# Moving a quad's attention scores behind the last block of attention's products in a gated cross-attention kernel, with dense 32x32 transposes and the gate bias added in DRAM

## The chip, the cores and the metric

The kernel runs on one core of a Trainium2 chip. The metric is device time in microseconds of the whole launch. Before the change it is 980.86 us, the median of three runs (980.78 to 980.89).

## The reference

Eight batches of 1024 tokens with 1024 features (`x`) attend to 64 memory rows of 512 features each. All is float32.

```python
memory_proj    = einsum('bme,de->bmd', memory, W_mem)            # 8 x 64 x 1024
scores         = einsum('bnd,bmd->bnm', x, memory_proj) / sqrt(1024)
attn           = softmax(scores, axis=-1)
memory_context = einsum('bnm,bmd->bnd', attn, memory_proj)
gate           = sigmoid(einsum('bnf,df->bnd', concat([x, memory_context]), W_gate) + b_gate)
fused          = x + gate * memory_context
out            = fused * rsqrt(mean(fused**2, -1) + 1e-6) * norm_w
```

Most of the work is the first half of the gate: x times a 1024 x 1024 weight, for 8192 tokens. The second half is small in another form: memory_context times W2 is attn times (memory_proj times W2), so the kernel computes `mg = memory_proj W2` once (512 x 1024), adds the bias to it (rows of attn sum to one), and multiplies attn by it.

## The kernel before, in words

**Stages.** A start of about 84 us loads the weights, projects the memory (`pm`), computes mg in seven block products (`mg_product`), and stores memory_proj and mg in two DRAM tensors, `mpd` and `mgd`. Then the tokens go through in 16 *quads* of 512 tokens, two a batch. A quad takes about 55 us.

**A quad.** x of the quad is loaded (`load_xq`) and transposed in blocks of 32x32 on VectorE (`transpose_x`), into four tiles A11, A12, A21, A22 of 256 tokens by 512 features. The 512 x 1024 by 1024 x 1024 product is then done by a fast scheme of seven block products in place of eight, on two levels. On the outer level VectorE forms sums S1 to S4 of the A tiles (`outer_s`); S3 is formed in place of A21. Each of the seven *blocks* is again seven *products* A, B, C, D, A, E, F (A has two parts), for which GpSimd forms four sums (`inner_s`). A product is two float32 matmuls, and the profile shows each as two records. So a quad has 49 products, one for each *slot*. VectorE and GpSimd add products into the `gate` tiles.

**Attention.** Scores of a quad (`scores`) are 16 float32 matmuls with 64 stationary columns each, two of them side by side on the array (tile psT, 32 records). ScalarE copies them to `sT`, TensorE turns them back (`transpose_scores`), softmax runs in two parts (`softmax_a`, `softmax_b`), and the result is turned once more (`transpose_attn`). Four of the seven blocks, those of outer products 5, 4, 2 and 3, are *extended*: after their second A product come eight matmuls of 64 rows, two side by side, with attn as the stationary side. They give memory_context (`pc`) and add mg's part of the gate to the block's sums (kA, kD, kE, kF). Sigmoid, gated product, residual (a DMA that adds x), and the norm follow.

**Order of the work.** Every engine's instructions stay in the order in which the program issues them (`pin`). That order is made by hand: `at(slot, fn)` issues a piece of work just before the product of a slot, `mid((quad, block), fn)` issues it inside a block, after its second A product and its extension, and ahead of the adds of that block and of product E (the loop over `beside` in `outer_product`). `plan(q)` fills in both. The blocks run in the order of `ORDER`: 1, 6, 7, 5, 4, 2, 3; the last number of a bracket says which half of the mg rows is used.

```python
ORDER = ((1, None), (6, None), (7, None), (5, (1, 1, 2)), (4, (1, 0, 2)), (2, (0, 0, 0)), (3, (0, 1, 4)))
SLOTS = 49
```

So block 1 has slots 0 to 6, block 6 slots 7 to 13, and block 3, the last, slots 42 to 48. In the kernel before, the scores of a quad and S3, S4 are issued at its slot 7, between blocks 1 and 6; S1 and S2 of the next quad in the middle of block 3.

**PSUM.** The products of a block use five banks that rotate from block to block (`banks`): a bank written in one block is written again, in the next block, four or more products after the matmuls that filled it, and must have been read by then. The extension's pc tiles have two banks of their own, and psT, the scores turned back and attn turned back share one (tag `sc`).

**Layout.** Token tiles are loaded so that a partition holds 32 tokens' quarter rows. In the kernel before, feature chunk j of a token holds features j, j + 8, j + 16, ...: `chunks` reads them with a step of eight floats, and the rows of both gate weights and the columns of W_mem are taken in the same way (`rows_by_chunk`, `chunks`).

**Bias.** mg's rows for a batch come back from `mgd` by `load_mg`; for each batch `add_bias` then adds b_gate to one half of them in SBUF, with a DMA from GpSimd's queue.

Of the kernel before, what the change touches and what calls it, by code (L numbers as in the profile page):

```python
# [10 lines left out]
ALU = mybir.AluOpType  # L11
# [4 lines left out]
P = 128  # L16
# [4 lines left out]
def tile_gated_cross_attention_rmsnorm(  # L21
# [38 lines left out]

    nc = tc.nc
    B, N, D = x.shape
    M, E = mem.shape[1:]
    QT = 4 * P
    QPB = N // QT
    NQ = B * QPB
    BM = B * M  # L70
    KD = D // P
    KE = E // P
    H = 512
    C = 256
    NPAIR = BM // P
# [6 lines left out]
    apool = ctx.enter_context(tc.tile_pool(name="apool", bufs=1))  # L82
# [6 lines left out]
    pin = tc.keep_in_program_order  # L89
# [7 lines left out]
    def load(o, i):  # L97
        pin(nc.sync.dma_start(o, i))

    def t4k(pool, shape, tag, name):  # L100
        return pool.tile(shape, F32, tag=tag, name=name)

    def rows_by_chunk(w, n):

        return w.rearrange("(p j) f -> p j f", j=n)

    def chunks(t, n):

        return t.rearrange("p s e -> p (s e)").rearrange("p (m j) -> p j m", j=n)

    banks = [f"b{i}" for i in range(5)]

    def bank(n, shape, name):
        return ps.tile(shape, F32, tag=banks[n % 5], name=name)
# [10 lines left out]
    memq = [t4k(rot, [P, 2, E], "l2", f"memq{i}") for i in range(2)]  # L125
    wm = t4k(xqpool, [P, KE, D], "xq", "wm")
    wmr = w_mem_t.rearrange("(k p) d -> p k d", p=P)
# [2 lines left out]
        load(memq[g], memr[g])  # L130
    load(wm[:, 1, :], wmr[:, 1, :])
    load(wm[:, 2:, :], wmr[:, 2:, :])
    w2r = rows_by_chunk(w_gate_t[D:, :], KD)
    w2 = []
    for k in range(KD):
        t = t4k(*((gpool, [P, D], "gate") if k < 7 else (apool, [P, D], "s4")), f"w2_{k}")
        load(t, w2r[:, k, :])
        w2.append(t)

    w1 = [const.tile([P, 4, D], F32, name=f"w1_{h}") for h in range(2)]
    for h in range(2):
        load(w1[h], rows_by_chunk(w_gate_t[:D, :], KD)[:, 4 * h : 4 * h + 4, :])
    nw_sb = const.tile([P, D], F32, name="nw_sb")
    load(nw_sb, norm_w.partition_broadcast(P))
    xq = {}

    def load_xq(q):
# [7 lines left out]
    outer_b = {  # L157
        o: w1[h][:, :, c * H : (c + 1) * H]
        for o, h, c in ((1, 0, 0), (7, 0, 1), (2, 1, 0), (3, 1, 1))
# [24 lines left out]
    mgd = dram.tile([2, BM, D], F32, name="mgd")  # L184
    memT = [t4k(rot, [P, 2, BM], "u", f"memT{i}") for i in range(2)]

    def transpose_mem(g):

        cols = slice(g * (BM // 2), (g + 1) * (BM // 2))
        for k in range(KE):  # L190
            for r in range(2):
                n = 2 * g + r
                pin(
                    nc.tensor.transpose(
                        pt[k][:, n * P : (n + 1) * P], memq[g][:, r, k * P : (k + 1) * P], ident
                    )
                )
            o = memT[k // 2][:, k % 2, cols]
            pin((nc.scalar.copy if k % 2 else nc.vector.tensor_copy)(o, pt[k][:, cols]))

    pt = [bank(4, [P, BM], "pt0")]
    pt += [ps_ctx.tile([P, BM], F32, tag="ctx", name=f"pt{k}") for k in (1, 2)]
    pt += [ps.tile([P, BM], F32, tag="sc", name="pt3")]
    for g in range(2):
        transpose_mem(g)
    pm = [bank(j, [P, BM], f"pm{j}") for j in range(5)]
    pm += [ps_ctx.tile([P, BM], F32, tag="ctx", name=f"pm{j}") for j in (5, 6)]
    pm += [ps.tile([P, BM], F32, tag="sc", name="pm7")]
    for k in range(KE):
        for j in range(KD):  # L210
            mm(
                pm[j],
                chunks(wm[:, k : k + 1, :], KD)[:, j],
                memT[k // 2][:, k % 2, :],
                k == 0,
                k == KE - 1,
            )
# [16 lines left out]
    A, S, L2, O = {}, {}, {}, {}  # L234
    sTs, attns, attnTs, scs, mps, mgs = {}, {}, {}, {}, {}, {}
# [3 lines left out]
    def transpose_x(q, t, half):  # L239

        key = q, t // 2, half
        if key not in A:
            A[key] = t4k(
                apool, [P, KH, 2 * P], f"a{t // 2 + 1}{half + 1}", f"a{t // 2 + 1}{half + 1}_{q}"
            )
        r = t % 2
        pin(
            nc.vector.transpose(  # L248
                A[key][:, :, r * P : (r + 1) * P],
                chunks(xq[q][:, 4 * t : 4 * t + 4, :], KD)[:, half * KH : (half + 1) * KH],  # L250
            )
        )

# [114 lines left out]
        for g in range(2):  # L368
            load(mgs[b][g * M : (g + 1) * M, :], mgd[g, b * M : (b + 1) * M, :])

    def add_bias(b):
        pin(nc.gpsimd.dma_start(mgs[b][M:P, :], b_gate.partition_broadcast(M), accum_op=ALU.add))

    KH = KD // 2
    HM = BM // 2
    b11, b12, b21, b22 = (
        [w2[h * KH + k][:, c * H : (c + 1) * H] for k in range(KH)]
# [17 lines left out]
    mpT = [[t4k(apool, [P, KH, HM], f"a{r + 1}{h + 1}", f"mpT{r}{h}") for h in range(2)] for r in range(2)]  # L397
# [14 lines left out]
    def store_mp(g):  # L412

        r, n = g // 2, g % 2
        mpq = const.tile([P, 4, Q4], F32, tag=f"it{(4, 6, 2, 3)[g]}", name=f"mpq{g}")
        for h in range(2):
            pin(
                nc.vector.transpose(
                    chunks(mpq, KD)[:, h * KH : (h + 1) * KH],
                    mpT[r][h][:, :, n * P : (n + 1) * P],  # L420
                )
            )
        for i in range(4):
            load(
                mgd[0, g * P : (g + 1) * P, i * Q4 : (i + 1) * Q4].rearrange(
                    "(s c) e -> c s e", c=32
                ),
                mpq[32 * i : 32 * (i + 1), :, :],
            )
# [16 lines left out]
    def mg_tile(pool, tag, name):  # L446
        return t4k(pool, [P, 2, H], tag, name)

# [10 lines left out]
    s1 = mp_step(nc.vector, "s1", apool, m21, m22, ALU.add)  # L459
    s2 = mp_step(nc.vector, "s2", apool, s1, m11, ALU.subtract)  # L460
# [59 lines left out]
    def at(slot, fn, *args):  # L520
        due.setdefault(slot, []).append(lambda: fn(*args))

    def mid(key, fn, *args):
        beside.setdefault(key, []).append(lambda: fn(*args))
# [5 lines left out]
    def plan(q):  # L530
        t0 = SLOTS * q
        nxt = q + 1 < NQ
        order = [o for o, _ in ORDER]
        for i, o in enumerate(order):
            for part, t in ((0, 1), (1, 5)):
                if i + 1 < len(order):
                    at(t0 + 7 * i + t, inner_s, q, order[i + 1], part)
                elif nxt:
                    at(t0 + 7 * i + t, inner_s, q + 1, order[0], part)
        at(t0 + 7, scores, q)  # L540
        at(t0 + 7, outer_s, q, 3)
        at(t0 + 7, outer_s, q, 4)
        at(t0 + 9, transpose_scores, q)
        at(t0 + 10, softmax_a, q)
        at(t0 + 13, softmax_b, q)
        at(t0 + 18, transpose_attn, q)
        at(t0 + 21, attn_difference, q)
        if not nxt:
            at(t0 + 5, load_last)
            return  # L550
        at(t0 + 2, load_xq, q + 1)
        for t in (2, 3):
            mid((q, 5), transpose_x, q + 1, t, 0)
            mid((q, 2), transpose_x, q + 1, t, 1)
        for i, t, half in ((36, 0, 0), (38, 1, 0), (43, 0, 1), (45, 1, 1)):
            at(t0 + i, transpose_x, q + 1, t, half)
        mid((q, 3), outer_s, q + 1, 1)
        mid((q, 3), outer_s, q + 1, 2)
        if (q + 1) % QPB == 0:
            at(t0 + 10, load_mp, (q + 1) // QPB)  # L560
            at(t0 + 49, load_mg, (q + 1) // QPB)
        if q % QPB == 0:
            at(t0 + 8, add_bias, q // QPB)

    for o in (2, 3):
        w1_place(o)
# [102 lines left out]
    def outer_product(q, o, ext):  # L669
# [3 lines left out]
        s1, s2, s3, s4 = (L2[q, o][:, i, :, :] for i in range(4))  # L673
# [64 lines left out]
        if ext:  # L738
            row, h, g = ext
# [43 lines left out]
        if o in (4, 3) and q + 1 == NQ:  # L783
            c, d = 2 * ext[0], 2 * ext[0] + 1
            if o == 3:
                sqrt_table()
            first = (4, 5) if o == 4 else (3, 3)
            at(slot + first[0], last_root, d)
            at(slot + first[1], last_root, c)
            for i, t in enumerate((d, c)):  # L790
                for h_ in range(2):
                    at(slot + first[1] + 1 + 2 * i + h_, last_norm, t, h_)
        elif o in (4, 3):

            row = ext[0]
            c, d = 2 * row, 2 * row + 1
            for t in (d, c):
                at(slot + 5, residual, q, t)
            if row == 0:
                when = (17, 18, 23, 29, None, None)  # L800
            else:
                when = (17, 18, 23, 25, 26, 28)
            at(slot + when[0], square, q, c)
            at(slot + when[1], square, q, d)
            for w_, (t, h_) in zip(when[2:], ((c, 0), (c, 1), (d, 0), (d, 1))):
                if w_ is None:
                    mid((q + 1, 4), norm, q, t, h_)
                else:
                    at(slot + w_, norm, q, t, h_)
# [36 lines left out]
```

## Time and profile before

| what | value |
|---|---|
| time | 980.86 us (980.78 to 980.89) |
| span of the profiled execution | 979.4 us |
| granted TensorE clock | 0.996 |
| VectorE: transposes of x | 128 of 128x512, 1098 ns each, 137.9 us |
| VectorE: S3 in place of A21 | 16, idle 23.2 us before them |
| TensorE: psT | 512 records, from quad to quad 55.05 us apart |
| GpSimd: bias | 8 DMAs of 256 KB, 847 ns of GpSimd each |
| DMA | 128.32 MB, 131 GB/s over the span |

How to read it: PE is TensorE's matmuls, PEld its weight loads, DVE VectorE, ACT ScalarE, POOL GpSimd, SP the engine that issues most DMAs. A group is a line of the code with its tiles, how many instructions it has, their busy time, the mean of one in ns, and the idle time of the engine just before them. Matmul ends are modelled in the profile and neighbours overlap, so for TensorE the times from start to start say more than busy time. `64*128` in a TensorE line is the tile of the array in use: rows by columns.

### The profile page before, as it was taken

What the parts mean: (1) busy time and instruction counts of PE and PEld (TensorE: products, weight loads), DVE (VectorE), ACT (ScalarE), POOL (GpSimd) and SP (SyncE); (2) the same over time, 40 slices, a digit from 0 to 9 for tenths busy, and PEclk for the clock granted to TensorE, in tenths of its full rate; (3) what the DMA queues carried; (4) which work ended last, traced back from release to release, by engine and by line L of the source; (5) the groups of instructions that cost most, each with busy time, mean ns of one, the idle gap of its engine ahead of it and who ended that gap; (6) DMA issues with size and microseconds to landing.
All of it is one profiled execution on the core that took longest, in us unless ns stands there. A gap on an engine that the chain in (4) does not pass through costs nothing.

```text
span 979.4 us, 14277 instructions
## 1 busy us (share of the span) xinstructions
PE 964.8 (99%) x4938; PEld 769.8 (79%) x4938; DVE 820.4 (84%) x1487; ACT 324.9 (33%) x602; POOL 730.5 (75%) x881
## 2 busy tenths in 40 slices
PE   9999999999999999999999999999999999999995
PEld 6546888888887888888887888888887888888873
DVE  3888788979797988979797988979797988979787
ACT  1100234151433334151433334151433334151434
POOL 3366877878787877878787877878787877878772
PEclk9999999999999999999999999999999999999998
DMA  9865264482918374482918374482818364482612
GB/s 372 258 153 145 39 120 107 103 188 62 186 65 165 108 141 106 102 190 65 183 65 164 111 138 105 107 184 66 182 65 168 110 136 104 108 184 68 169 65 86
DMA packets 71255, 128.32 MB, mean 131 GB/s; under 512 B 12432, under 2 KB 49296, under 8 KB 70928
## 3 DMA queue, kind: packets, MB, share of 16 engines
q1 hardware_dynamic: 61760, 93.34, 35.3%
q0 software_dynamic: 9280, 33.56, 18.5%
q8 instruction: 39, 0.64, 0.3%
q10 hardware_dynamic: 144, 0.52, 0.2%
q14 instruction: 32, 0.26, 0.1%
HBM read 87.56 MB, written 39.85 MB: 130 GB/s over the span
## 4 chain that ended last, share of the span: by engine, by line
PE 96%; DVE 2%; DMA 1%; issue 0%; ACT 0%; POOL 0%; DVEq 0%; ACTq 0%
PE kA L92 20%; PE pc L92 12%; PE kE L92 11%; PE kF L92 10%; PE kD L92 10%; PE kC L92 10%; PE kB L92 10%; PE psT L92 6%; PE pg L92 5%; PE pm L92 3%; DVE gate L95 1%; DMA memq<-in_mem 1%; DVE gate L660 0%; PE pa L342 0%; PE sc L316 0%
## 5 line engine op out<-in xcount | busy, mean ns | idle before, releaser
L95 POOL TENSOR_TENSOR gate<-gate,u 128x256 f32<-128x256 f32 x336 | 270.4, 835 | 115.7 <-DVE u L95 110.1
L582 ACT ACTIVATE gate<-gate 128x512 f32<-128x512 f32 x128 | 79.0, 629 | 400.1 <-DVE gate L95 400.1
L95 POOL TENSOR_TENSOR l<-a 128x256 f32<-128x256 f32 x128 | 128.9, 1007 | 60.4 <-DVE a L95 55.8
L248 DVE STREAM_TRANSPOSE a<-xq 128x512 f32<-128x512 f32 x128 | 137.9, 1098 | 4.0 <-DMA xq<-in_x 4.0
L92 PE MATMUL pc<-mg,attnT 64*128 64x256 f32 x512 | 127.4, 389 | 0.0
L611 DVE SCALAR_TENSOR_TENSOR gate<-gate,ss,nw_sb 128x512 f32<-128x512 f32 x120 | 126.0, 1060 | 1.1
L92 PE MATMUL kD<-it,l 128*128 128x256 f32 x448 | 115.0, 379 | 0.0
L92 PE MATMUL kB<-it,l 128*128 128x256 f32 x448 | 115.0, 379 | 0.0
L92 PEld LDWEIGHTS pc<-mg,attnT 64*128 64x128 f32 x512 | 90.6, 186 | 29.7 <-issue 21.2
L92 PE MATMUL kA<-w,a 128*128 128x256 f32 x384 | 98.7, 379 | 0.4 <-ACT u L726 0.4
L92 PEld LDWEIGHTS kD<-it,l 128*128 128x128 f32 x448 | 85.1, 190 | 11.6
L92 PEld LDWEIGHTS kB<-it,l 128*128 128x128 f32 x448 | 85.1, 190 | 11.6
L95 DVE TENSOR_TENSOR gate<-gate,pc 128x512 f32<-128x512 f32 x128 | 87.0, 680 | 5.8 <-ACT gate L582 5.8
L95 POOL TENSOR_TENSOR l<-s 128x256 f32<-128x256 f32 x96 | 75.7, 789 | 10.8 <-PE kF L92 10.7
L92 PEld LDWEIGHTS kA<-w,a 128*128 128x128 f32 x384 | 71.6, 190 | 10.2 <-ACT u L726 0.8
L726 ACT COPY u<-kA 128x256 f32<-128x256 f32 x112 | 40.5, 362 | 102.1 <-PE kA L92 99.9
L92 PE MATMUL kE<-it,a 128*128 128x256 f32 x256 | 69.0, 392 | 0.0
L95 DVE TENSOR_TENSOR u<-u,kB 128x256 f32<-128x256 f32 x112 | 45.5, 406 | 28.1 <-PE kB L92 24.9
L92 PE MATMUL kA<-t,s 128*128 128x256 f32 x256 | 67.4, 386 | 0.0
L92 PE MATMUL kC<-w,l 128*128 128x256 f32 x256 | 65.7, 379 | 0.0
L92 PE MATMUL kF<-w,l 128*128 128x256 f32 x256 | 65.7, 379 | 0.0
L596 ACT ACTIVATE junk<-gate 128x1024 f32<-128x1024 f32 x60 | 63.5, 1059 | 2.1 <-DMA gate<-in_x 1.2
(123 smaller groups left out, 1996.6 us busy)
## 6 DMA issues: line engine op xcount, KB each, us to landing
xq<-in_x SPq DMA_DIRECT2D x64, 512.0 KB, 9.6
gate<-in_x POOLq DMA_DIRECT2D x60, 512.0 KB, 7.8
out<-gate SPq DMA_DIRECT2D x60, 512.0 KB, 2.6
w<-in_w_gate_t SPq DMA_DIRECT2D x8, 512.0 KB, 11.0
w<-in_w_gate_t SPq DMA_DIRECT2D x2, 2048.0 KB, 15.6
mg<-mgd SPq DMA_DIRECT2D x16, 256.0 KB, 4.0
mpd<-mpT SPq DMA_DIRECT2D x4, 512.0 KB, 3.8
mgd<-mpq SPq DMA_DIRECT2D x16, 128.0 KB, 2.6
```

The source lines that it names most:

```text
L92: pin(nc.tensor.matmul(o, lhsT, rhs, start=start, stop=stop, skip_group_check=True))
L95: pin(eng.tensor_tensor(o, a, b, op))
L248: nc.vector.transpose(A[key][:, :, r * P : (r + 1) * P], chunks(xq[q][:, 4 * t : 4 * t + 4, :], KD)[:, half * KH : (half + 1) * KH],)
L582: pin(nc.scalar.activation(g, g, AF.Sigmoid))
L596: nc.scalar.activation(junk, O[q, t], AF.Square, accum_out=ss[:, t % 2 : t % 2 + 1])
L611: nc.vector.scalar_tensor_tensor(g[:, cols], g[:, cols], rstd[:, t % 2 : t % 2 + 1], nw_sb[:, cols], ALU.mult, ALU.mult,)
L726: pin(nc.scalar.copy(p1, kb["A"]))
```

## The change

The change has five parts:

1. *Scores.* For quads 1 to 15 the scores are issued inside block 3 of the quad before, right behind attention's matmuls there. Quad 0 keeps them at slot 7. S3 and S4 go from slot 7 to slots 5 and 6 (but for quad 0).
2. *Dense blocks.* Feature chunk j becomes 32 features in a row out of each quarter of 256. `blocks` and `tokens` then read and write runs of 32 floats in both kinds of transposes (of x and of memory_proj). The gate weights' rows are loaded in that order: w2 in eight loads as before, w1 in eight of 512 KB where it was two of 2 MB. The columns of W_mem are put in order by four copies on VectorE (`order_wm`), from which the projection then reads its stationary side.
3. *Bias.* For batch 0 it is added as before. For batches 1 to 7 one DMA adds it to the 448 rows of `mgd`, in quad 0 at slot 20.
4. *Transposes.* Two of the eight transposes of the next quad go from slots 43 and 45 to 42 and 43.
5. *Norms.* The last two norm halves of the row finished in block 4 go from 26 and 28 to 29 and 32 slots after it, which are slots 15 and 18 of the next quad.

Parts 1, 4 and 5 set the order on TensorE and VectorE, part 2 is meant to make VectorE's transposes read and write dense memory, and part 3 is to take issues off GpSimd.

```diff
-    def rows_by_chunk(w, n):
-        return w.rearrange("(p j) f -> p j f", j=n)
-    def chunks(t, n):
-        return t.rearrange("p s e -> p (s e)").rearrange("p (m j) -> p j m", j=n)
+    def rows_by_chunk(w):
+        return w.rearrange("(i j r) f -> i r j f", i=4, r=32)
+    def blocks(t, half):
+        return t.rearrange("p s (j r) -> p s j r", r=32)[:, :, half * KH : (half + 1) * KH, :]
+    def tokens(t):
+        return t.rearrange("p j (s c) -> p s j c", c=32)
...
-    for h in range(2):
-        load(w1[h], rows_by_chunk(w_gate_t[:D, :], KD)[:, 4 * h : 4 * h + 4, :])
+    for k in range(KD):
+        load(w1[k // KH][:, k % KH, :], w1r[:, :, k, :])
...
+    def order_wm(k):
+        t = t4k(apool, [P, KD, P], ("a11", "a12", "s1", "s2")[k], f"wmp{k}")
+        pin(
+            nc.vector.tensor_copy(
+                t.rearrange("p j (i r) -> p j i r", r=32),
+                wm[:, k, :].rearrange("p (i j r) -> p j i r", i=4, r=32),
+            )
+        )
+        wmp.append(t)
+    order_wm(0)
     for g in range(2):
         transpose_mem(g)
+    for k in range(1, KE):
+        order_wm(k)
...
             nc.vector.transpose(
-                A[key][:, :, r * P : (r + 1) * P],
-                chunks(xq[q][:, 4 * t : 4 * t + 4, :], KD)[:, half * KH : (half + 1) * KH],
+                tokens(A[key][:, :, r * P : (r + 1) * P]),
+                blocks(xq[q][:, 4 * t : 4 * t + 4, :], half),
             )
...
-        at(t0 + 7, scores, q)
-        at(t0 + 7, outer_s, q, 3)
-        at(t0 + 7, outer_s, q, 4)
+        if q == 0:
+            at(t0 + 7, scores, q)
+        at(t0 + (5 if q else 7), outer_s, q, 3)
+        at(t0 + (6 if q else 7), outer_s, q, 4)
...
-        for i, t, half in ((36, 0, 0), (38, 1, 0), (43, 0, 1), (45, 1, 1)):
+        for i, t, half in ((36, 0, 0), (38, 1, 0), (42, 0, 1), (43, 1, 1)):
             at(t0 + i, transpose_x, q + 1, t, half)
+        mid((q, 3), scores, q + 1)
         mid((q, 3), outer_s, q + 1, 1)
         mid((q, 3), outer_s, q + 1, 2)
...
-        if q % QPB == 0:
-            at(t0 + 8, add_bias, q // QPB)
+        if q == 0:
+            at(t0 + 8, add_bias, mgs[0][M:P, :])
+            at(t0 + 20, add_bias, mgd[1, M:, :])
...
-                when = (17, 18, 23, 25, 26, 28)
+                when = (17, 18, 23, 25, 29, 32)
```

More of the change, by code (lines that the diff above doesn't have):

```diff
@@ L72, in tile_gated_cross_attention_rmsnorm @@
     KE = E // P
+    KH = KD // 2
     H = 512
@@ L132, in tile_gated_cross_attention_rmsnorm @@
     load(wm[:, 2:, :], wmr[:, 2:, :])
-    w2r = rows_by_chunk(w_gate_t[D:, :], KD)
+    w2r = rows_by_chunk(w_gate_t[D:, :])
     w2 = []
@@ L136, in tile_gated_cross_attention_rmsnorm @@
         t = t4k(*((gpool, [P, D], "gate") if k < 7 else (apool, [P, D], "s4")), f"w2_{k}")
-        load(t, w2r[:, k, :])
+        load(t, w2r[:, :, k, :])
         w2.append(t)
     w1 = [const.tile([P, 4, D], F32, name=f"w1_{h}") for h in range(2)]
-    for h in range(2):
-        load(w1[h], rows_by_chunk(w_gate_t[:D, :], KD)[:, 4 * h : 4 * h + 4, :])
+    w1r = rows_by_chunk(w_gate_t[:D, :])
+    for k in range(KD):
+        load(w1[k // KH][:, k % KH, :], w1r[:, :, k, :])
     nw_sb = const.tile([P, D], F32, name="nw_sb")
@@ L203, in tile_gated_cross_attention_rmsnorm @@
     pt += [ps.tile([P, BM], F32, tag="sc", name="pt3")]
+    wmp = []
+    def order_wm(k):
[8 more added lines that the diff above has]
+    order_wm(0)
     for g in range(2):
         transpose_mem(g)
+    for k in range(1, KE):
+        order_wm(k)
     pm = [bank(j, [P, BM], f"pm{j}") for j in range(5)]
@@ L212, in tile_gated_cross_attention_rmsnorm @@
                 pm[j],
-                chunks(wm[:, k : k + 1, :], KD)[:, j],
+                wmp[k][:, j, :],
                 memT[k // 2][:, k % 2, :],
@@ L369, in load_mg, with add_bias @@
             load(mgs[b][g * M : (g + 1) * M, :], mgd[g, b * M : (b + 1) * M, :])
-    def add_bias(b):
-        pin(nc.gpsimd.dma_start(mgs[b][M:P, :], b_gate.partition_broadcast(M), accum_op=ALU.add))
-    KH = KD // 2
+    def add_bias(rows):
+        pin(
+            nc.gpsimd.dma_start(
+                rows, b_gate.partition_broadcast(rows.shape[0]), accum_op=ALU.add
+            )
+        )
     HM = BM // 2
@@ L418, in store_mp @@
                 nc.vector.transpose(
-                    chunks(mpq, KD)[:, h * KH : (h + 1) * KH],
-                    mpT[r][h][:, :, n * P : (n + 1) * P],
+                    blocks(mpq, h),
+                    tokens(mpT[r][h][:, :, n * P : (n + 1) * P]),
                 )
```

## The prediction

> **What bounds the kernel now.** I read the page first (busy times, the chain that ended last), then TensorE's waits, then TensorE's timeline in one quad of the middle, and last the groups and the timeline of the engines that the change relieves. The page's busy row and the chain:
>
> ```profile
> PE 964.8 (99%) x4938; PEld 769.8 (79%) x4938; DVE 820.4 (84%) x1487; ACT 324.9 (33%) x602; POOL 730.5 (75%) x881
> ...
> PE 96%; DVE 2%; DMA 1%; issue 0%; ACT 0%; POOL 0%; DVEq 0%; ACTq 0%
> ```
>
> TensorE is the chain. Busy ends are modelled, so I asked its waits too. They come to 3.9 us in all; the largest:
>
> ```profile
> PE kA L92 <- ACT u L726: 1.6, 3, 1.1
> ```
>
> Three waits, all in the last quad. The psT groups of quads 1 to 15 start at 145.77, 200.81, 255.86, ... us: 55.05 us apart every time. So each quad is as long as TensorE's own stream, and only what shortens that stream, or makes it wait, moves the time. Now the stream. Its timeline around the scores of one quad (start, length, both in us):
>
> ```profile
> 420.04 1.03 PE L92 MATMUL kF<-w,l 128*128 128x256 f32 x4
> 421.00 3.67 PE L92 MATMUL psT<-a,mpb 128*64 128x256 f32 x32
> 424.60 1.13 PE L92 MATMUL kA<-t,s 128*128 128x256 f32 x4
> 425.57 1.03 PE L92 MATMUL kB<-it,l 128*128 128x256 f32 x4
> ```
>
> A product is four records, 0.864 us from start to start where nothing changes (400.25, 401.12, 401.98 in the same view), that is 0.216 a record. Here the tile of the array changes: 128*128, then 128*64, then 128*128. kF's successor is due at 420.04 + 0.864 = 420.90 and comes at 421.00: 0.10 late. The 16 pairs of psT take 16 x 0.216 = 3.456, so kA is due at 424.46 and comes at 424.60: 0.14 late. kB is due at 424.60 + 0.864 = 425.46 and comes at 425.57: 0.11 late. Going into the scores and out of them costs 0.35 us.
>
> The same view around attention's products in block 2 (64 rows of the array, two side by side):
>
> ```profile
> 401.98 1.03 PE L92 MATMUL kA<-w,a 128*128 128x256 f32 x4
> 402.94 0.48 PE L92 MATMUL pc<-mg,attnT 64*128 64x256 f32 x1
> ...
> 403.26 0.38 PE L92 MATMUL pc<-mg,attnT 64*128 64x256 f32 x1
> ...
> 404.86 1.13 PE L92 MATMUL kE<-it,a 128*128 128x256 f32 x4
> 405.83 1.03 PE L92 MATMUL kF<-w,l 128*128 128x256 f32 x4
> ```
>
> Entry: pc comes 0.10 after its due 402.84, and the second pair 0.32 after the first instead of 0.216: 0.20 together. Exit: the last pair starts at 404.55, so kE is due at 404.77 and comes at 404.86, and kF is 0.11 late: 0.20. Four such blocks a quad and one of scores; each has an entry and an exit.
>
> [...]about 0.10 us at each of the ten changes a quad. [...] The strided reads here step 32 bytes; pm's weight loads show it in the groups below, 314 ns against 190 for dense ones (kB's).
>
> ```profile
> L248 DVE STREAM_TRANSPOSE a<-xq 128x512 f32<-128x512 f32 x128 | 137.9, 1098 | 4.0 <-DMA xq<-in_x 4.0
> ...
> L95 DVE TENSOR_TENSOR a<-a,a 128x1024 f32<-128x1024 f32 x16 | 20.0, 1251 | 23.2 <-PE psT L92 23.2
> ...
> L92 PEld LDWEIGHTS pm<-memT,wm 128*128 128x128 f32 x64 | 20.0, 314 | 7.3
> ```
>
> **The change, part by part.**
>
> *Scores of the next quad behind attention's products of block 3.* In the order of instructions the 32 psT records stand between the last mg record and kE, for quads 1 to 15; quad 0 keeps its place. Before, the two blocks cost 0.40 + 0.35 = 0.75. After: entry of the mg block 0.20, one change from 64*128 straight to 128*64, exit to 128*128 0.20. The trace has no such direct change. Its lower bound is [...]0.14, as from 128*128; its upper bound is that it costs like an exit and an entry, 0.34. I take 0.14[...]. After: 0.54, so 0.20 saved per quad (0.197 in ns) and 15 x 0.20 = 3.0 us. At the upper bound nothing is saved.
>
> Does psT wait for data there? Its last inputs are the transposes of slots 43 and 45, now 42 and 43. Before, the last of these ended at 411.26 in the quad where mg's products ran from 411.1 to 412.8. Now kF's add ends at 407.39 as before, then come transpose, gated product, transpose at 0.69, 0.68, 0.69: done at 409.5, over 3 us ahead. No wait. ACT's copy of psT then stands before the sigmoids of that block, which wait for later matmuls anyway: nothing.
>
> *S3, S4 at products 5 and 6; and what lay behind psT.* Moving psT takes 3.6 us from between products 6 and 7, and gives them to VectorE in block 3. This is where a wait could arise, for softmax stands in products 9 to 13. VectorE there, before:
>
> ```profile
> 420.24 0.42 DVE L95 TENSOR_TENSOR gate<-u,kE 128x256 f32<-128x256 f32 x1 [0.97 <-PE kE L92]
> 421.11 0.42 DVE L95 TENSOR_TENSOR gate<-u,kF 128x256 f32<-128x256 f32 x1 [0.44 <-PE kF L92]
> 423.00 1.23 DVE L95 TENSOR_TENSOR a<-a,a 128x1024 f32<-128x1024 f32 x1 [1.47 <-PE psT L92]
> 424.14 1.22 DVE L95 TENSOR_TENSOR s<-a,s 128x1024 f32<-128x1024 f32 x1
> 426.71 0.42 DVE L95 TENSOR_TENSOR u<-u,kB 128x256 f32<-128x256 f32 x1 [1.35 <-PE kB L92]
> ```
>
> S3 (a<-a,a) waited for psT, which reads the same tile: 1.47 us here, 23.2 in all. Idle in these rows: 0.97 + 0.44 + 1.47 + 1.35 = 4.2 us, against 3.6 that go. Laid out again: the add before ends at 419.27, S3 runs to 420.5, kE's add to 420.9, S4 to 422.1, kF's add to 422.5. kB of block 6 would be ready at 426.6 - 3.6 = 423.0. So VectorE arrives with 0.5 us to spare and enters block 6 as it did. From there two norm halves (0.9 to 1.2 us each) go from products 12, 14 to 15, 18, where it has gaps of 0.23 to 0.26 us between adds. Behind S4 stands kF's add, 1.0 us later than before; its bank is next written in block 6's product E, five products (4.3 us) on. A bank lies four products, 3.5 us, between its last matmul and its next. Cost: 0.
>
> GpSimd needs S3 for block 7; it waited 3.7 us for it (420.57 to 424.30) and now waits none. Cost: 0.
>
> *Dense transposes.* 128 of 1.098 us. [...] The nearest dense row, the 128x512 add, takes 0.69. I take 0.69: 128 x 0.41 = 52 us off VectorE[...]. It lies beside TensorE's stream, so none of it is on the path. Even with 1.1 us kept, the gated product ahead of block 3's pc would end at about 411.2 with its matmul at 411.1: a tenth of a us at stake.
>
> *Copies of wm (order_wm).* Four of 128x1024; [...]1.22 (the 128x1024 add). The first stands ahead of memT's copies, which began at 6.68. Its data had landed at 4.99, and an arrival is used some 0.8 us after the last byte (memq: 5.37, first use 6.23), so it runs from 5.8 to [...]7.0 (0.35 us, on the path). The others run beside pm's 27 us. Dense weight loads: hidden behind a 0.43 us matmul, but for pm's second record, 0.66 after the first: -0.1. Sum of the start: -0.1 to +0.35; I take 0.
>
> *Bias in DRAM; w1 in eight loads; norms.* Seven issues of 0.85 us leave GpSimd; one of 448 rows comes in quad 0, and needs to land only before quad 2, more than 70 us later. w1's chunks go in the same order with the same bytes, 2.5 us a MiB. None is on the path: 0. The last quad (its TensorE waits of 2.1 us, its 10 us tail) stays.
>
> **The rivals.** *VectorE becomes the bound* (slower). Against: the 0.5 us left over above, 84% busy now and less after. For: an add of 0.4 us too late in each quad is enough, 15 x (0.4 - 0.2) = +3, 984; one S block too late (1.2) would be 996. *The direct change costs as two do*: 980.9. For: no record of it. Against: every change in the trace costs the same 0.10 whatever the two modes. *More goes*: a faster VectorE also frees the last quad's waits (2.1) and one of 0.3 in quad 0: 975.5. Against: these follow squares and residual adds that the change leaves.
>
> **The numbers.** 980.86 - 3.0 + 0.0 = 977.9. Chances: this 0.79, VectorE bound 0.09, direct change dear 0.07, more 0.05. The main case spans 977.2 to 978.6 (start, rounding); the range goes to 976.4 toward the fourth and 980.2 for a dearer change. Faster by over 0.2% means below 978.9.
>
> **What would show it.** psT groups 54.85 us apart (55.05 now); psT 0.10 late after mg and 0.05 more at its second pair; no a<-a,a wait on psT; STREAM_TRANSPOSE near 0.69; TensorE's waits no larger. Wrong would be new rows "PE <- DVE" in every quad, or a mg-to-psT change of 0.2 or more.

## The result, and the profile after

The changed kernel takes 1035.63 us (1033.54 to 1036.94, five runs) against 980.87 us before: a ratio of 1.0556, with a 95% interval of 1.0540 to 1.0571. I had forecast 977.9 us. The span grew from 979.4 to 1033.8 us, 54.4 us, and nearly all of it lies ahead of the first quad.

The page of the changed kernel: busy times, TensorE's busy tenths in 40 slices of 26 us each, GB/s in the same slices, and the chain that ended last.

```profile
PE 971.1 (94%) x4938; PEld 763.5 (74%) x4938; DVE 793.8 (77%) x1491; ACT 326.7 (32%) x602; POOL 734.8 (71%) x875
...
PE   9309899999999999999999999999999999999995
...
GB/s 184 104 105 211 137 173 72 168 88 130 115 137 98 122 144 106 150 78 172 68 183 61 172 93 157 90 127 123 128 110 107 159 93 162 66 179 63 177 67 82
...
PE 85%; SPq 5%; DVE 4%; DMA 4%; issue 1%; ACT 0%; POOL 0%; DVEq 0%; ACTq 0%
```

TensorE's busy time is near that of before (971.1 against 964.8 us), but its second and third slices are nearly empty, and a DMA queue (SPq, DMA: 9%) has come into the chain. Before, the first slices moved 372 and 258 GB/s; now they move 184, 104 and 105. TensorE's waits in the changed kernel (waiting engine, what released it, us in total, times, longest):

```profile
PE pg L92 <- ACT mpT L424: 41.5, 1, 41.5
PE pg L92 <- DVE w L95: 4.8, 2, 4.3
PE kB L92 <- DVE gate L95: 2.4, 1, 2.4
```

One wait of 41.5 us: mg's first product wants mpT, a copy of the projection. VectorE and ScalarE share these copies, and ScalarE's waits in turn for VectorE's. Why that one is late is seen on VectorE, whose timeline in the start has these rows (start, length, idle before and what ended it):

```profile
16.67 0.69 DVE L95 TENSOR_TENSOR t_w<-w 128x512 f32<-128x512 f32 x1 [4.54 <-DMA w<-in_w_gate_t]
21.69 0.69 DVE L95 TENSOR_TENSOR t_w<-w 128x512 f32<-128x512 f32 x1 [4.32 <-DMA w<-in_w_gate_t]
...
71.77 2.29 DVE L95 TENSOR_TENSOR t<-w 128x2048 f32<-128x2048 f32 x1 [19.21 <-DMA w<-in_w_gate_t]
...
76.51 2.74 DVE L424 COPY mpT<-pm 128x256 f32<-128x256 f32 x8
```

Before the change the same view had:

```profile
12.57 0.69 DVE L95 TENSOR_TENSOR t_w<-w 128x512 f32<-128x512 f32 x1 [3.69 <-DMA w<-in_w_gate_t]
13.86 0.69 DVE L95 TENSOR_TENSOR t_w<-w 128x512 f32<-128x512 f32 x1 [0.59 <-DMA w<-in_w_gate_t]
...
31.16 0.75 DVE L400 COPY mpT<-pm 128x256 f32<-128x256 f32 x2
```

VectorE's sums of the gate weights stand ahead of the mpT copies in its queue. Each 512 KB of weights now arrives 5.02 us after the one before (16.67, 21.69, ...); before the change it was 1.28 us (12.57, 13.86, ...). The last of the projection's matmuls starts at 35.3 (35.8 before), and its result lies there until 76.5. The first quad's first product starts at 134.9 instead of 84.3: 50.6 us. Besides the 41.5 these are 4.8 us of waits for another sum of weights, and some 4.3 us of slower mg products right behind the two pauses: TensorE's granted clock was 0.75 from 77.4 to 86.6 us and 0.82 from 118.6 to 128.0, against 1.00 over the same products before.

The same stretch of the start as a window, before the change and after it. The columns are the stretch, its length, the busy time of PE, PEld, DVE, ACT and POOL, TensorE's clock, the mean busy share of the 16 DMA engines, and GB/s. Before:

```profile
12.00:27.00 15.00, 15.00 (x36) 10.95 (x36) 8.31 (x9) 0.00 (x0) 6.82 (x4) 1.00 1.04 428
```

After:

```profile
20.00:70.00 50.00, 15.87 (x37) 6.67 (x36) 4.85 (x7) 0.00 (x0) 7.09 (x4) 0.71 0.26 105
```

A quarter of the engines' time, and a quarter of the bytes a second. The trace also keeps every packet that a DMA engine moves, for these loads one row each. In this stretch four packets were in flight for nine tenths of the time, and a 4 KB packet took 159 ns; before, from 12 to 27 us, it was sixteen or more throughout, and 164 ns. So these are not slow engines, but four of sixteen.

The quads. TensorE's timeline of the changed kernel where attention's products of block 3 meet the scores:

```profile
355.69 0.38 PE L92 MATMUL pc<-mg,attnT 64*128 64x256 f32 x1
...
356.00 3.67 PE L92 MATMUL psT<-a,mpb 128*64 128x256 f32 x32
359.61 1.13 PE L92 MATMUL kE<-it,s 128*128 128x256 f32 x4
360.58 1.03 PE L92 MATMUL kF<-w,l 128*128 128x256 f32 x4
```

psT is due 0.216 after the last pair, at 355.91, and comes at 356.00: 0.09 late, what each of the ten changes a quad cost before, and 0.05 more at its second pair (356.27), as before (421.00, 421.27). That change is as cheap as I had taken it. But the psT groups stand 55.11 us apart, not 54.85, for TensorE now waits in block 7 of every quad:

```profile
318.63 1.03 PE L92 MATMUL kA<-w,a 128*128 128x256 f32 x4
319.66 1.13 PE L92 MATMUL kB<-it,l 128*128 128x256 f32 x4
320.62 1.03 PE L92 MATMUL kC<-w,l 128*128 128x256 f32 x4
```

kB comes 1.03 after kA instead of 0.864, and kC 0.96 after kB: 0.16 for the wait and 0.10 at kB's second record, which comes 0.32 after its first, not 0.216. kA's weight load started 0.21 ahead of its first matmul (318.42, 318.63); kB's starts with it (319.65, 319.66). kB takes over the PSUM bank of block 6's kD, and its weight load starts when VectorE has added that kD:

```profile
319.19 0.41 DVE L95 TENSOR_TENSOR gate<-gate,kD 128x256 f32<-128x256 f32 x1
319.65 0.73 PEld L92 LDWEIGHTS kB<-it,l 128*128 128x128 f32 x4 [0.40 <-DVE gate L95]
```

VectorE has no gap from 310.0 to that add. Earlier in this stretch, in block 1 and at the start of block 6:

```profile
310.65 2.39 DVE L95 TENSOR_TENSOR a<-a,a 128x1024 f32<-128x1024 f32 x1
312.96 0.41 DVE L95 TENSOR_TENSOR gate<-u,kE 128x256 f32<-128x256 f32 x1
313.29 1.70 DVE L95 TENSOR_TENSOR s<-a,s 128x1024 f32<-128x1024 f32 x1
314.92 0.41 DVE L95 TENSOR_TENSOR gate<-u,kF 128x256 f32<-128x256 f32 x1
315.25 0.41 DVE L95 TENSOR_TENSOR u<-u,kB 128x256 f32<-128x256 f32 x1
```

S3 and S4 take 2.39 and 1.70 us, not the 1.23 and 1.22 of before. GpSimd's timeline shows what runs beside S3:

```profile
310.22 1.05 POOL L95 TENSOR_TENSOR l<-s 128x256 f32<-128x256 f32 x1
310.91 1.04 POOL L95 TENSOR_TENSOR l<-s,l 128x256 f32<-128x256 f32 x1
```

In the quad of before that the prediction reads, GpSimd had:

```profile
418.85 1.05 POOL L95 TENSOR_TENSOR l<-s 128x256 f32<-128x256 f32 x1
419.54 1.04 POOL L95 TENSOR_TENSOR l<-s,l 128x256 f32<-128x256 f32 x1
424.30 1.64 POOL L95 TENSOR_TENSOR l<-a 128x256 f32<-128x256 f32 x1 [3.73 <-DVE a L95]
```

There S3 waited for psT until 423.00; the two sums were over by 420.58, and the next one waited for S3. Nobody was beside it. The two sums took as long there, with little on VectorE, so beside S3 it is VectorE that loses, not GpSimd. In the changed kernel S3 ends 1.09 us after GpSimd's second sum (313.04 and 311.95), and S4 1.08 us after the end of the sum beside which it starts (314.99 and 313.91); each takes some 1.23 alone. GpSimd's spans are rough, and why S3 is slow beside these sums was not shown.

The groups that answer to those shown of before:

```profile
L269 DVE STREAM_TRANSPOSE a<-xq 128x512 f32<-128x512 f32 x128 | 85.9, 692 | 8.8 <-DMA xq<-in_x 8.8
L95 DVE TENSOR_TENSOR a<-a,a 128x1024 f32<-128x1024 f32 x16 | 37.1, 2318 | 0.9 <-PE psT L92 0.9
...
L92 PEld LDWEIGHTS pm<-memT,wmp 128*128 128x128 f32 x64 | 12.1, 190 | 14.8 <-issue 14.8
...
L215 DVE COPY wmp<-wm 128x1024 f32<-128x1024 f32 x4 | 2.7, 689 | 5.5 <-DMA wm<-in_w_mem_t 5.5
```

The dense transposes and pm's dense weight loads cost what dense rows of before had shown (0.69 us for the 128x512 add, 190 ns for kB's loads): 692 and 190 ns. A copy of wm costs 689, not the 1.22 us of the 128x1024 add. S3's wait for psT is gone, but for quad 0.

The 54.4 us: the start 50.6; from the first product of kA to the last 3.2 more (883.4 against 880.2); the tail 0.6. The 3.2 are about -3.0 for the array changes, +3.9 for the waits of kB in 15 quads, and +2.6 for one long wait of kB in quad 0, ahead of 154.4, in place of one of 0.3. Ahead of that long wait VectorE has

```profile
149.79 3.86 DVE L95 TENSOR_TENSOR it<-w,it 128x512 f32<-128x512 f32 x1
```

where such a sum takes 0.69 alone. GpSimd's adds run one behind the other from 148.71 to 153.10 here, and the sum ends 0.55 us after the last of these: the same picture as for S3, and the strongest case of it.

### The profile page after: what moved, and what is told of

Same layout as the page of the kernel before. It is cut to its first block, busy times and chain, and to the rows that moved or that the text cites. A ratio compares the mean times of both kernels' runs of the same rounds, so it can differ in the third digit from the quotient of the medians.

```text
span 1033.8 us, 14297 instructions
## 1 busy us (share of the span) xinstructions
PE 971.1 (94%) x4938; PEld 763.5 (74%) x4938; DVE 793.8 (77%) x1491; ACT 326.7 (32%) x602; POOL 734.8 (71%) x875
## 4 chain that ended last, share of the span: by engine, by line
PE 85%; SPq 5%; DVE 4%; DMA 4%; issue 1%; ACT 0%; POOL 0%; DVEq 0%; ACTq 0%
PE kA L92 18%; PE pc L92 11%; PE kE L92 10%; PE kB L92 10%; PE kF L92 9%; PE kD L92 9%; PE kC L92 9%; PE psT L92 6%; SPq L98 5%; DMA w<-in_w_gate_t 2%; PE pg L92 2%; DVE gate L95 1%; DMA xq<-in_x 1%; DVE w L95 1%; DVE t L95 0%
## 5 line engine op out<-in xcount | busy, mean ns | idle before, releaser
L95 POOL TENSOR_TENSOR gate<-gate,u 128x256 f32<-128x256 f32 x336 | 290.8, 896 | 106.1 <-DVE u L95 106.1
L638 DVE SCALAR_TENSOR_TENSOR gate<-gate,ss,nw_sb 128x512 f32<-128x512 f32 x120 | 121.9, 1026 | 1.1
L95 POOL TENSOR_TENSOR l<-a 128x256 f32<-128x256 f32 x128 | 98.2, 767 | 27.2 <-DVE a L95 18.5
L95 POOL TENSOR_TENSOR l<-s 128x256 f32<-128x256 f32 x96 | 79.1, 824 | 48.5 <-PE kF L92 47.6
L95 DVE TENSOR_TENSOR gate<-gate,kE 128x256 f32<-128x256 f32 x112 | 45.5, 418 | 69.7 <-PE kE L92 66.2
L269 DVE STREAM_TRANSPOSE a<-xq 128x512 f32<-128x512 f32 x128 | 85.9, 692 | 8.8 <-DMA xq<-in_x 8.8
L95 POOL TENSOR_TENSOR l<-l,a 128x256 f32<-128x256 f32 x64 | 68.1, 1064 | 5.0
L92 PE MATMUL pg<-w,mpT 128*128 128x512 f32 x48 | 25.5, 683 | 46.4 <-ACT mpT L424 41.5
L95 DVE TENSOR_TENSOR gate<-gate,kF 128x256 f32<-128x256 f32 x112 | 45.8, 418 | 26.4 <-PE kF L92 19.0
## 6 DMA issues: line engine op xcount, KB each, us to landing
mgd<-mpq SPq DMA_DIRECT2D x16, 128.0 KB
```

What stands on the lines that cost most here:

```text
L92: pin(nc.tensor.matmul(o, lhsT, rhs, start=start, stop=stop, skip_group_check=True))
L95: pin(eng.tensor_tensor(o, a, b, op))
L269: nc.vector.transpose(tokens(A[key][:, :, r * P : (r + 1) * P]), blocks(xq[q][:, 4 * t : 4 * t + 4, :], half),)
L638: nc.vector.scalar_tensor_tensor(g[:, cols], g[:, cols], rstd[:, t % 2 : t % 2 + 1], nw_sb[:, cols], ALU.mult, ALU.mult,)
```

## The experiments

Theory 1, put to the 0.26 and the four packets above: a load whose slowest dimension is 4, here 4 groups of 32 rows, runs on 4 of the 16 DMA engines. Theory 2: the wait in block 7 comes from S3 and S4 being slowed by GpSimd (2.39 and 1.70 us). Rivals: the copies of wm or the new order make the start slow; the new row order or small packets are slow; norms or GpSimd's sums make the wait.

### The loads alone, on the kernel before

```diff
-        return w.rearrange("(p j) f -> p j f", j=n)
+        return w.rearrange("(i j r) f -> i r j f", i=4, r=32)
...
-        load(t, w2r[:, k, :])
+        load(t, w2r[:, :, k, :])
...
-    for h in range(2):
-        load(w1[h], rows_by_chunk(w_gate_t[:D, :], KD)[:, 4 * h : 4 * h + 4, :])
+    w1r = rows_by_chunk(w_gate_t[:D, :], KD)
+    for k in range(KD):
+        load(w1[k // 4][:, k % 4, :], w1r[:, :, k, :])
```

> The kernel before, with the gate weights loaded in the new pattern (4 groups of 32 rows named as two dimensions in one DMA; w2 in eight loads, w1 in eight) and nothing else changed. The weights' rows then stand in another order than x's features, so the output is another one. Theory 1 (a load whose slowest dimension is 4 runs on 4 of the 16 DMA engines, so 512 KB take 5.0 us instead of 1.3): the start grows by some 50 us as in the changed kernel, 1030 us in all. Rival A (the start is slow for the copies of wm or something else that the change does on VectorE): 981 us.

Measured: 1035.53 us. The first product of quad 0 starts at 138.2, and from 20 to 70 us the window gives 0.26 of the DMA engines and 105 GB/s again. The quads stand 55.05 apart, as before. So the loads alone make the start slow, and neither wm's copies nor the order is needed for it. That the total is the changed kernel's is chance: here the start is 53.9 us longer and the quads are as before, there the start is 50.6 longer and the quads take 3.2 more.

### w1 in eight loads, old rows

```diff
-    for h in range(2):
-        load(w1[h], rows_by_chunk(w_gate_t[:D, :], KD)[:, 4 * h : 4 * h + 4, :])
+    w1r = rows_by_chunk(w_gate_t[:D, :], KD)
+    for k in range(KD):
+        load(w1[k // 4][:, k % 4, :], w1r[:, k, :])
```

> The kernel before, with w1 in eight loads of 512 KB (rows of 4 KB) instead of two of 2 MB (rows of 16 KB), in the old row order. Theory 1: these loads keep their 128 rows as one dimension, so nothing changes, 980.8 us. Rival B (packets of 4 KB, or more issues, slow the start): up to some us more.

Measured: 981.53 us, ratio 1.0006 (0.9997 to 1.0015): no difference that this run can tell. Eight loads of 4 KB rows are not the cause.

### Two groups of 32 rows in a load

```diff
-        load(t, w2r[:, :, k, :])
+        for i in range(2):
+            load(t[64 * i : 64 * (i + 1), :], w2r[2 * i : 2 * i + 2, :, k, :])
...
-        load(w1[k // KH][:, k % KH, :], w1r[:, :, k, :])
+        for i in range(2):
+            load(w1[k // KH][64 * i : 64 * (i + 1), k % KH, :], w1r[2 * i : 2 * i + 2, :, k, :])
```

> The changed kernel with each weight load split in two DMAs of 64 rows, each of 2 groups of 32. Theory 1 (the slowest dimension sets how many DMA engines share a load: 4 with 4 groups, so 2 with 2 groups): 256 KB take 5 us as 512 KB did, the weights take 160 us instead of 80, 1035 + some 80 = 1110 to 1120 us. Rival E (each group costs a fixed time, or the row order is slow): 1035 us, or less.

Measured in one run: 1115.53 us. The window of its start:

```profile
20.00:130.00 110.00, 15.94 (x38) 6.74 (x36) 5.54 (x8) 0.00 (x0) 7.08 (x4) 0.59 0.13 52
```

0.13 of sixteen engines is two, at 52 GB/s: half of the changed kernel's 0.26 and 105. Two packets are in flight for 95% of this stretch, and a 4 KB packet takes 159 ns as in the changed kernel. With 4 groups four engines work, with 2 groups two, each as fast as before. This is the measurement that settles theory 1 for 4 groups and for 2: the rows and their order are the same in both, and two packets nearly without a gap are not what a fixed time for each load or group would leave. Busy shares of the engines that the runs show: 0.13 with 2 groups, 0.26 with 4, 1.04 with 32 rows (the next run) or 128 (the kernel before).

### 32 rows in a load

```diff
-        load(t, w2r[:, :, k, :])
+        for i in range(4):
+            load(t[32 * i : 32 * (i + 1), :], w2r[i, :, k, :])
...
-    for k in range(KD):
-        load(w1[k // KH][:, k % KH, :], w1r[:, :, k, :])
+    for h in range(2):
+        for i in range(4):
+            load(w1[h][32 * i : 32 * (i + 1), :, :], w1r[i, :, h * KH : (h + 1) * KH, :])
```

> The changed kernel, with each weight load split into four DMAs of 32 rows each (w1: four per half, 512 KB each), the same rows to the same places. Theory 1: each DMA's slowest dimension is 32, all 16 DMA engines share it, the start is back at some 84 us, and what remains is the quads: 980.9 - 15 x 0.20 (one array change less) + 15 x 0.27 (a wait of kB in block 7) = 982 us. Rival B (it is the new row order, 32 neighbouring rows of 4 KB, or packets of 4 KB in place of 16 KB, that memory serves slowly): still above 1020 us.

Measured: 993.23 us, ratio 1.0127 (1.0112 to 1.0142). Neither number came. All engines work again, as theory 1 has it, but at half the rate, 225 GB/s against 428, as the window shows, and the start ends at 95.4, 11.1 us later than before:

```profile
12.00:40.00 28.00, 23.82 (x56) 10.26 (x54) 6.76 (x10) 0.00 (x0) 7.10 (x4) 0.99 1.04 225
```

The quads stand 55.11 apart, as in the changed kernel, so the wait in block 7 has nothing to do with the start.

### 32 partitions in a load, old rows

The kernel before, its loads split as in the last experiment:

```diff
-        load(t, w2r[:, k, :])
+        for i in range(4):
+            load(t[32 * i : 32 * (i + 1), :], w2r[32 * i : 32 * (i + 1), k, :])
...
-        load(w1[h], rows_by_chunk(w_gate_t[:D, :], KD)[:, 4 * h : 4 * h + 4, :])
+        for i in range(4):
+            p = slice(32 * i, 32 * (i + 1))
+            load(w1[h][p], w1r[p, 4 * h : 4 * h + 4, :])
```

> The kernel before with its old row order, and each weight load split into DMAs of 32 partitions, as e2_loads32 does with the new order. It tells why e2_loads32 and e6_two_queues move a MiB in 4.6 us with all DMA engines busy. Theory 3b (32 partitions at a time are what halves the rate, whatever the rows): some 230 GB/s again, the start about 11 us longer, 991 us. Rival F (32 neighbouring rows of 4 KB, that is 128 KB of memory in one piece, are read at half the rate): 415 GB/s as before, 981 to 983 us.

Measured: 992.46 us, and

```profile
12.00:40.00 28.00, 23.93 (x56) 16.97 (x55) 6.42 (x9) 0.00 (x0) 7.12 (x4) 1.00 1.04 226
```

226 GB/s with the old rows, 225 with the new, where 128 partitions at a time had 428: 32 at a time halve the rate, and the row order has no part in it. The packets themselves are slow: one of 4 KB takes 279 ns (median; 162 in the kernel before), one of 16 KB 1261 (615). What is added grows with the bytes (117 and 646 ns), so it is not a fixed cost of each row or each load.

### Two queues for two halves of the partitions

```diff
+    def load_act(o, i):
+        pin(nc.scalar.dma_start(o, i))
...
-        load(t, w2r[:, :, k, :])
+        for i in range(2):
+            load(t[32 * i : 32 * (i + 1), :], w2r[i, :, k, :])
...
+    def upper_half():
+        for k in range(KD):
+            for i in (2, 3):
+                load_act(w2[k][32 * i : 32 * (i + 1), :], w2r[i, :, k, :])
...
+    upper_half()
     for k in range(1, KE):
         order_wm(k)
```

> The changed kernel with its weight loads split into DMAs of 32 rows as in e2_loads32, those for partitions 0 to 63 issued on SyncE's queue and those for 64 to 127 on ScalarE's, behind the memory's transposes. Theory 3 (in e2_loads32 a MiB took 4.6 us and not 2.5, for all DMA engines wrote into the same 32 partitions at a time, which take half of what 128 take): two groups of partitions are written at a time, the start loses most of its 11 us, 982 to 986 us. Rival D (short DMAs or this row order are slow in themselves): 990 us or more.

Measured: 993.24 us. From 15 to 40 us the engines are full (1.04) at 241 GB/s, little better than 225, though both queues are served in that stretch (690 and 780 packets of 4 KB). Only from 34 to 43 us, with w1's 512 KB halves in flight, is it 288 GB/s against 213 with one queue. Theory 3 has failed as I put it: two halves on two queues do not bring the 428 GB/s of 128 partitions back. Why loads of 32 partitions move half as much stays open.

### The order alone

The kernel before with parts 1, 4 and 5 of the change: scores, S3 and S4, two transposes, two norm halves (their lines of the change's diff).

> The kernel before, with only the order changed: scores behind attention's products of block 3, S3 and S4 at slots 5 and 6, the two transposes and the two norm halves moved. Strided transposes (1.10 us), the old loads and the bias for each batch stay. Theory 2: the saving of 0.20 us a quad and the wait of kB are both there, 982 us or somewhat more; if the 1.10 us transposes make VectorE late ahead of block 3's attention products as well, 983 to 986. If the dense transposes did not matter for TensorE at all: the same as e2_loads32.

Measured: 981.78 us, ratio 1.0011 (1.0004 to 1.0017). The quads stand 55.06 to 55.12 us apart (one 55.30), with kB's wait in each. So the saving of 0.20 a quad and a wait of 0.26 cancel, and it comes out 1 us slow. The transposes here take 1.10 us: that the changed kernel's take 0.69 changes nothing for TensorE.

### S4 late

As the changed kernel with loads of 32 rows, and:

```diff
-        at(t0 + (6 if q else 7), outer_s, q, 4)
+        at(t0 + (20 if q else 7), outer_s, q, 4)
```

> As e2_loads32, and S4 of quads 1 to 15 formed at slot 20 instead of slot 6 (it is needed from slot 36 on). Theory 2 (kB of block 7 waits since S3 and S4, 4.1 us together with the slowing by GpSimd, push VectorE's add of kD in block 6 past the bank's next use): 1.7 us go from VectorE ahead of that add, the wait of 0.16 + 0.10 us a quad is gone, the psT groups stand 54.85 us apart, 977.9 us. Rival C (the wait comes from the norms at products 15 and 18 or from GpSimd's sums): 982 us as e2_loads32.

My 977.9 was written before I knew that loads of 32 rows cost 11 us; what this run tells is the distance of the quads. Measured: 992.29 us, quads 55.03 to 55.05 apart (one 54.93). kB waits no more. But a new wait of 0.20 (0.10 ahead of kC and 0.10 at its second record) stands in block 5. GpSimd there:

```profile
448.77 1.70 POOL L95 TENSOR_TENSOR l<-s 128x256 f32<-128x256 f32 x1
450.43 0.91 POOL L95 TENSOR_TENSOR l<-s,l 128x256 f32<-128x256 f32 x1
```

The first sum takes 1.70 instead of 0.73, while S4 runs on VectorE from 448.49 for 1.40. kC needs it and starts at 450.53. The wait had moved to the other engine: here S4 started first, and GpSimd's sum is the one that loses most (0.97 us, S4 0.18).

### GpSimd's sums out of S3's way

As the order alone, with

```diff
-            for part, t in ((0, 1), (1, 5)):
+            for part, t in ((0, 1), (1, 5 if i or q == 0 else 3)):
```

> As e4_order_only, with GpSimd's last two sums for block 6 of quads 1 to 15 issued at slot 3 instead of slot 5, ahead of two DMA issues, so that they are done before S3 starts at slot 5. VectorE's order is that of e4_order_only. Theory 2 (S3 takes 2.4 us and not 1.23 since GpSimd reads and writes SBUF beside it, and that alone makes the add of kD late): S3 takes some 1.25 us, the wait of kB in block 7 is gone, psT groups 54.85 us apart, 977.6 to 979 us. Rival H (S3 is slow for another reason, such as psT's or the DMA's reads, or the add is late even so): S3 2.3 us, 981.8 us.

Measured: 979.90 us, ratio 0.9988 (0.9980 to 0.9997). VectorE's order is that of the order alone; only GpSimd's two sums end before S3 starts. S3's group in this kernel:

```profile
L95 DVE TENSOR_TENSOR a<-a,a 128x1024 f32<-128x1024 f32 x16 | 19.9, 1244 | 1.2 <-PE psT L92 1.2
```

1.24 us where the order alone has 2.33; S4, too, is at 1.22 instead of 1.70 from quad 1 on. kB waits in block 7 of no quad, where it waited in fifteen of the order alone, and nine of the fourteen distances from quad 1 on are 54.85. This shows theory 2: S3 and S4 are slow because of GpSimd's sums beside them, and that made kD's add late; the moved norms, which stand as in the order alone, do not make the wait. The other five distances are 0.3 to 1.2 us longer. They fall in quads that begin a batch, where GpSimd has a bias DMA to issue, and the waits there stand at other products.

### S3 behind psT

As the order alone, with

```diff
-        at(t0 + (5 if q else 7), outer_s, q, 3)
+        if q == 0:
+            at(t0 + 7, outer_s, q, 3)
...
         mid((q, 3), outer_s, q + 1, 2)
+        at(t0 + 47, outer_s, q + 1, 3)
```

> As e4_order_only (the kernel before with only the order changed), and S3 of the next quad formed at slot 47 of block 3, behind the adds of kA and kD, where VectorE was idle for 3 us while psT ran and GpSimd was idle too. Theory 2 (S3 and S4 at slots 5 and 6 cost VectorE 4.1 us just ahead of softmax, since GpSimd's sums run beside them, and this makes the add of kD late for its bank): S3 takes 1.25 us again, no wait of kB is left, the psT groups stand 54.85 us apart, 980.8 - 15 x 0.20 - 0.3 = 977.6 us. Rival C (norms or GpSimd's sums make the wait): 981.8 us as e4_order_only.

Measured: 978.92 us (978.02 to 980.50), ratio 0.9979 (0.9972 to 0.9987). Most quads stand 54.85 apart, as expected; the total misses 977.6 by 1.3; in the profiled run two quads have 0.3 too much, again from waits at other products. S3 takes 1.76 there, not the 1.25 expected, and S4, with less beside it, 1.25.

### The bias in DRAM on top

The last kernel, with part 3 of the change.

> As e5_order_s3at47, and the bias of batches 1 to 7 added to the rows in DRAM by one DMA in quad 0. Theory 2: seven issues of 0.85 us leave GpSimd, which TensorE does not wait for once S3 is moved: the same as e5_order_s3at47, 978.9 us, within 0.3. Rival G (the issues delay GpSimd's sums in the quads that start a batch, and the waits of 0.3 us that e5_order_s3at47 still has in three quads come from that): up to 1 us less.

Measured: 977.92 us (977.87 to 978.03), ratio 0.9970 (0.9959 to 0.9981). All fourteen distances from psT of quad 1 on are 54.85. TensorE's waits:

```profile
PE kA L92 <- ACT u L735: 1.7, 3, 1.1
PE pz L92 <- DVE zeros L118: 1.2, 1, 1.2
```

Rival G holds: without the seven bias issues on GpSimd the time is 2.90 us below that of the kernel before, where the last run was 2.03 below it, and the runs no longer scatter. The issues cost 0.9 us in all. This version is 0.3% faster than the kernel before, with the strided transposes and the old loads.

## Why the prediction was wrong

**The bound** stands for the quads: TensorE's stream set the time of each, and the chain said so truly. In the start of the changed kernel it is the loads.

**One array change less, 0.20 a quad** stands. psT comes 0.09 to 0.10 late after mg; where nothing else waits the quads stand 54.849 apart instead of 55.047, 0.198 each, 3.0 us in 15. That the direct change costs as one and not as two was my estimate, for the trace of before has no such change; all 15 of the changed kernel come 0.09 late, and 0.05 more at the second pair. The last experiment gives 980.82 - 977.92 = 2.9. Its time is the 977.9 of the forecast, but it is another kernel, with S3 elsewhere and the old loads: that the two agree does not make the forecast right.

**"w1's chunks go in the same order with the same bytes, 2.5 us a MiB. None is on the path: 0"** is the step that failed, by 50 us. The order and bytes are the same, but the rate is not: 10.0 us a MiB, measured (5.02 per 512 KB). I carried a rate from one access pattern to another. The prediction looks at order and bytes, and not at how many DMA engines the load keeps busy (a share of 1.04 before, 0.26 after); w2's loads, which take the new pattern too, it does not price at all, and none of its rivals has slow loads in it. Once the rate is 10.0, 8 MiB take 80 us, and VectorE's queue, in which the sums of weights stand ahead of mpT's copies, hands that on to TensorE. My trace of before showed that queue with little to spare: its mpT copies began at 31.16, right after the last sum of w1.

**"VectorE arrives with 0.5 us to spare"** failed too, by 1.6 us a quad. I laid S3 and S4 out at 1.23 and 1.22, durations from a place where GpSimd waited for S3 itself. In the new place GpSimd works, and they take 2.39 and 1.70. I put S3 at 419.27 to 420.5 and named 420.57 as the end of GpSimd's work, and did not set the two side by side. The rival "VectorE becomes the bound" had the right place and a wait of the right kind; its size was 0.26 a quad against the 0.20 saved. It could have been seen, for the same trace had s<-a,a at 1.33 and s<-s,a at 1.60 with GpSimd beside them, for the same shape. The prediction also has GpSimd wait for S3 no more; it still waits 1.24 us for it (313.18 in the changed kernel).

**The dense transposes, the copies of wm** were worth for the time what I had said: none. The transposes were right in size (692 ns). A copy of wm takes 689 ns; that the first one costs nothing was my estimate, and no copy of its shape is in the trace of before. In the changed kernel it runs from 4.97 to 5.66, and memT's copies begin at 6.50.

**The bias** I had at zero. In the kernel before nothing speaks against it, for its quads stand 55.05 apart with a bias issue and without; with TensorE's stream tighter it was worth 0.9 us.

## What to carry to other kernels

A new access pattern for a load is a new load: before taking a measured rate over to it, measure it in its new form, and read the DMA share of the window beside the GB/s, for it can leave most DMA engines idle (0.26 busy with 4 groups of 32 rows here, 1.04 with 128 rows). A duration on VectorE belongs to its place as much as to its shape (1.24 to 2.39 us for one 128x1024 add here): when an instruction moves, ask what GpSimd does at the new place, and which of the two starts first. Where one engine's stream is the whole time, small fixed costs between its instructions are a real gain (0.198 us a quad here), but only if each engine that feeds it keeps what slack it had.

## What the runs showed that I had not expected

- 512 KB in 4 groups of 32 rows took 5.02 us and not 1.28; 4 groups kept 0.26 of the DMA engines busy, 2 groups 0.13.
- Loads of 32 partitions with all DMA engines busy move 225 to 226 GB/s, against 428 with 128, whatever the rows; spread over two queues and both halves of the partitions, 241 (288 in the last stretch).
- A 128x1024 add on VectorE takes 1.24 us alone and up to 2.39 beside GpSimd's adds, a 128x512 one 0.69 and once 3.86; GpSimd's 128x256 sum, beside an add of VectorE that started first, goes from 0.73 to 1.70.
- A TensorE wait of 0.16 us cost 0.26: kB's weight load started with its first matmul, and the second record came 0.32 after the first, not 0.216.
